# A convolutional row LSTM on one core: the work between the statistics and the first whole row is dealt out anew

## The chip, the core and the metric

The kernel runs on one core of a Trainium2 chip. The core has five engines that each work through a queue of their own in order: TensorE (PE in the profile, its weight loads PEld), VectorE (DVE), ScalarE (ACT), GpSimd (POOL) and SyncE (SP), which issues the transfers. They wait for each other on semaphores. The metric is the device time of one launch in microseconds; lower is better.

## The reference

The input `x` has 8 images of 96 channels and 128 x 128 pixels. The output is `x` plus a convolutional LSTM that runs over the 128 rows of each image from top to bottom, on the group-normalised input (32 groups of 3 channels, statistics over a whole image):

```python
its = lax.conv_general_dilated(X, W_is * mask, window_strides=(1, 1), padding=((0, 0), (1, 1)),
                               dimension_numbers=('NCHW', 'OIHW', 'NCHW')) + b_is[None, :, None, None]
def step(carry, row_in):
    h, c = carry
    ss = lax.conv_general_dilated(h, W_ss, window_strides=(1,), padding=((1, 1),),
                                  dimension_numbers=('NCW', 'OIW', 'NCW')) + b_ss[None, :, None]
    gates = ss + row_in
    g5 = gates.reshape(B, 3, 4, Oc, Wd)
    f, i, o = (jax.nn.sigmoid(g5[:, :, n].reshape(B, O, Wd)) for n in range(3))
    g = jnp.tanh(g5[:, :, 3].reshape(B, O, Wd))
    c_new = f * c + i * g
    h_new = o * jnp.tanh(c_new)
    return ((h_new, c_new), h_new)
_, hs = lax.scan(step, (h0, c0), xs)
return x + jnp.moveaxis(hs, 0, 2)   # X above is _gn(x)
```

A row can't begin before the row above it is done, so the rows are a chain of 128 steps. Both convolutions are three pixels wide along the row.

## The kernel before

**Half-steps.** The 8 images are two halves of 4, whose chains don't depend on each other. One row of one half is a half-step: half-step `n` is row `n // 2` of half `n % 2`, and there are 256 of them. While one half's products run on TensorE, the other half's gates run on ScalarE and VectorE. Four rows are a block. In the tile names the first digit behind the name is the half: `xs10` is half 1, buffer 0.

**Operands.** A row's even and odd pixels stand apart, and both convolutions are computed on sums and differences of neighbouring pixels. For the recurrent part these are made from the last hidden row `h`, which lies in `hx` beside 32 normalised input channels: the sum `vs` (step `S`, line 617) and the difference `vf` (step `F`, line 621), both on VectorE, and the shifted differences `vd` (step `D`, line 625) on GpSimd. `S` and `F` read two tiles in SBUF, as do all sums and differences here; the gates' VectorE instructions read one of their inputs from PSUM, where the products lie. For the other 64 input channels the sums and differences are made ahead of time, for whole blocks: `widen` (line 308 on ScalarE, 310 on GpSimd) normalises an image's 4 rows from `xr` into `xw`, `add_pixels` (line 327) writes the sums and `subtract_pixels` (line 331) the differences into `xs`. These three instructions on GpSimd are called an image below. The 32 channels in `hx` are normalised by `normalise_shared` (the same lines 308 and 310, written to `hx`).

**Products of a half-step.** The output channels come in three groups A, B and C of 128, one PSUM bank each. Group by group, `P` and `Q` are products with `xs`' sums and its first differences, `E` with its last ones; `1` and `2` take `vs` and `vf`, `0` and `3` take `vd`. Between them ScalarE copies the sum out (`cp`), and VectorE adds and subtracts the bank's halves (`lo`, `hi`). `E` of a group comes after its `lo`; `0` and `3` come after its `hi`. Then follow tanh (`ta`, line 555) and sigmoid (`si`), the products of the gates (`fg` for forget, line 572; `gt`, line 581), `ce`, `th`, the output `ou` that writes `h`, and the residual `re`, which adds `h` to `x`. A mark `+` or `*` behind a name means one or two half-steps ahead.

**Where the change acts.** The first 116 us read all of `x` for the statistics. Half-steps 0 and (in part) 2 already run beside that; the second half's last image comes last, and its scale is known at 135.3 us. From there to the regular rhythm the order is written out by hand: ScalarE widens rows 1 to 3 of block 0 of half 1 into `rows` (the buffer `piece0`), GpSimd normalises the shared channels of these rows and makes their sums and differences row by row (`own_row`), and `do(1, ...)` issues half-step 1 with the first products of half-steps 2 and 3. The residual of half-steps 0 and 1 runs on GpSimd. From half-step 2 on the string `PERIOD` sets the order, and GpSimd's share of each half-step comes from `work(n)`: normalised channels, one image for the next block, and a load. For the first 8 half-steps the table `FIRST` stands in for its rule; there the first image of half 1's block 1 is spread over three half-steps, in a second buffer `xw1`, and `LATER` spreads one image of block 2 over half-steps 9, 11 and 13.

**What a queue holds.** A wait on TensorE holds everything behind it in its queue. With 64 operand rows a product uses half of the array, and two such products run side by side in the two row groups; one with 128 rows needs both.

Of the kernel before, what the change touches and what calls it, by code (L numbers as in the profile page):

```python
# [21 lines left out]
def kernel(  # L22
# [29 lines left out]
    nc = tc.nc  # L52
    B, C, H, W = x.shape
    P = 128
    NH = 2
    BH = B // NH
    R = 4
    NB = H // R
    J = W // 2
# [80 lines left out]
    xw = [const.tile([P, R, W + 1], F32, tag=f"xw{i}", name=f"xw{i}") for i in range(2)]  # L140
# [11 lines left out]
    def rows_of(s, k, c0, c1, lo=0, hi=R):  # L152
        return x[s * BH : (s + 1) * BH, c0:c1, k * R + lo : k * R + hi, :].rearrange(
            "b c r w -> c b (r w)"
        )

    def load_rows(s, k, lo=0, hi=R):
        src = rows_of(s, k, 0, C2, lo, hi)
        for p in range(2):
            nc.sync.dma_start(xr[s][p * C2 : (p + 1) * C2, :, lo * W : hi * W], src)  # L160
# [10 lines left out]
    E = mybir.EngineType  # L171
# [140 lines left out]
    def widen(engine, xw, i, n, s, k, j, lo, step=1):  # L312


        return norm(
            engine,
            strided(xw[:, i, :], 0, [(step * (W + 1), n), (J + 1, 2), (1, J)]),
            xr[s][:, j, lo * W : (lo + n) * W]
            .rearrange("p (r j t) -> p r t j", r=n, t=2),
            0,  # L320
            1,
            s * BH + j,
        )

    def add_pixels(xw, n, total):

        nc.gpsimd.tensor_add(total, xw[:, 0:n, 0:J], xw[:, 0:n, J + 1 :])  # L327

    def subtract_pixels(xw, n, differences):

        nc.gpsimd.tensor_sub(  # L331
            differences,
            strided(xw[:, 0, :], 0, [(W + 1, n), (J, 2), (1, J)]),
            strided(xw[:, 0, :], J + 1, [(W + 1, n), (0, 2), (1, J)]),
        )

    def combine(xw, n, total, differences):

        add_pixels(xw, n, total)
        subtract_pixels(xw, n, differences)  # L340

    def own_image(s, k, j):

# [1 line left out]
        widen(nc.gpsimd, xw[0], 0, R, s, k, j, 0)  # L345
        combine(xw[0], R, to[:, :, 0, j, :], to[:, :, 1:3, j, :])

    def own_row(xw, s, r, lo=0, hi=BH):

        to = xs[s][0]  # L350
        combine(
            xw[:, lo:hi],
            hi - lo,
            to[:, r, 0, lo:hi],
            to[:, r, 1:3, lo:hi].rearrange("p t b j -> p b t j"),
        )

    def normalise_shared(engine, s, k, j, lo, hi):
# [17 lines left out]
    last = NT * NH - 1  # L376
# [63 lines left out]
    class HalfStep:  # L440
# [44 lines left out]
        def own(self, a, i):  # L485

            low = a == order["A"] or (a == order["C"] and (self.s == 0 or (self.n, i) == (1, 2)))
            rhs = self.xs[:, i].rearrange("p b j -> p (b j)")
            self.mm(a, i % 2, wo[i], rhs, slice(0, C2) if low else slice(C2, P))
# [94 lines left out]
        def part(self, ap, lo, hi, t=None):  # L584
            ap = ap.rearrange("p (t b j) -> p t b j", t=2, b=BH)
            return ap[:, :, lo:hi] if t is None else ap[:, t, lo:hi]
# [45 lines left out]
        def residual(self):  # L632
            s, row = self.s, self.row
            xo = xt[s, row // R][0:C, :, row % R, :].rearrange("p b (j t) -> p t b j", t=2)
            if self.n < NH or self.n == last - 1:
                nc.gpsimd.tensor_add(xo, xo, self.h)
            else:
                residuals.append(nc.vector.tensor_add(xo, xo, self.h))  # L638
# [21 lines left out]
    def shared(s, k, *images, engine=nc.gpsimd):  # L660
        parts = [j if isinstance(j, tuple) else (j, 0, R) for j in images]
        return [
            (normalise_shared, nc.scalar if hi == 1 else engine, s, k, j, lo, hi)
            for j, lo, hi in parts
        ]

    def beside(s, k, *images):
        return shared(s, k, *images, engine=nc.scalar)

    spread = own(1, 1, 0, 1)  # L670
    FIRST = [
        ([], own(0, 1, 0), []),
        (shared(0, 1, 0), own(0, 1, 1), []),
        (beside(0, 1, 1) + shared(0, 1, 2), own(0, 1, 2), []),
        (beside(0, 1, 3) + shared(1, 1, 0), own(0, 1, 3), [spread[0], (load_rows, 0, 2)]),
        (beside(1, 1, 1) + shared(1, 1, 2), own(1, 1, 1), [spread[1]]),
        (shared(1, 1, 3), own(1, 1, 2), [spread[2]]),
        ([], own(1, 1, 3), [(load_rows, 1, 2)]),
        ([], own(0, 2, 0), []),
    ]  # L680
    LATER = dict(zip((9, 11, 13), own(1, 2, 0, 1)))

    def work(n):
        if n < len(FIRST):
            return FIRST[n]
        row, s = divmod(n, NH)
        k, r = divmod(row, R)
        ahead, image = (k + 2, 0) if r == R - 1 else (k + 1, r + 1)
        return (
            shared(s, k + 1, *SHARED[r]) if k + 1 < NB else [],  # L690
            own(s, ahead, image) if ahead < NB else (),
            ([(load_rows, s, k + 2)] if r == R - 2 and k + 2 < NB else [])
            + ([LATER[n]] if n in LATER else []),
        )

    worked = {}
# [24 lines left out]
    def finish(n):  # L721
        prepare(n)
        row, s = divmod(n, NH)
        k, r = divmod(row, R)
        if r == R - 1:
            store(s, k, R - 1 if k + 1 == NB else 0, R)
            if k + 2 < NB:
                load(s, k + 2)
        elif r == R - 2 and k + 1 == NB:
            store(s, k, 0, R - 1)  # L730
# [26 lines left out]
    def half_step(n):  # L757
        if n not in steps:
            steps[n] = HalfStep(n)
        return steps[n]  # L760

    def do(n, names, by_lanes=False):

        for name in names.split():
            if name in "UX":
                if n >= NH:
                    prepare(n - NH, name)
                continue
            if name[0] == "W":
                prepare(n - 1 + name.count("+") - name.count("'"), name.strip("W+'"))  # L770
                continue
            at = n
            for mark, offset in (("'", -1), ("+", 1), ("*", 2)):
                at += offset * name.count(mark)
                name = name.replace(mark, "")
            images = None
            lane = "<>".find(name[-1]) if name[-1] in "<>" else None
            name = name.rstrip("<>")
            if name[0] in OWN and name[-1] in IMAGES:
                images, full = IMAGES[name[-1]], name[:-1]  # L780
# [39 lines left out]
    def shared_rows(engine, s, lo, hi, images=range(BH)):  # L820
        for j in images:
            normalise_shared(engine, s, 0, j, lo, hi)
# [97 lines left out]
    n = m = 0  # L920
# [38 lines left out]
    rows = ring[2][:, 0 : (R - 1) * BH * (W + 1)].rearrange("p (r q) -> p r q", q=W + 1)  # L959
# [28 lines left out]

    for j in range(BH):
        widen(nc.scalar, rows, j, R - 1, 1, 0, j, 1, step=BH)  # L990
    shared_rows(nc.gpsimd, 1, 1, R, range(0, 2))
    own_row(rows[:, 0:BH], 1, 1)
    shared_rows(nc.gpsimd, 1, 1, R, range(2, BH))
    for r in range(2, R):
        own_row(rows[:, (r - 1) * BH : r * BH], 1, r)
    load_rows(0, 1)
    for s in range(NH):
        load(s, 1)
    load_rows(1, 1)
# [2 lines left out]

    do(1, "1A 2A 1B 2B 1C 2C PA PB QA QB")
    half_step(1).images.clear()
    do(1, "E+A PC E+C QC P*A E+B cpA cpB cpC loA loB loC")
    do(1, "EA P*B Q*A EB EC Q*B hiB hiA hiC 0B 3B 0A 3A 0C 3C taB siB taA taC siC")
    finish(0)
    do(1, "gt th 0+A 3+A 0+B 3+B 0+C 3+C ou F S D re")
    finish(1)
# [65 lines left out]
```

## Time and profile before

| | us |
|---|---|
| median of 3 runs | 1966.7 |
| lowest, highest | 1965.13, 1968.21 |
| the profiled execution | 1967.33 |
| its span in the trace | 1965.5 |
| TensorE busy in the span | 1901.2 (97%) |
| VectorE, ScalarE, GpSimd busy | 1794.7, 1567.1, 1359.4 |

In the rows of the profile, "us from the span's start" comes first, then the duration, engine, line, operation and `out<-in` with partitions x elements; what ended the engine's idle time before the instruction stands in brackets at the end. One product shows up as two matmul records and two weight loads. An instruction's start can lie some tenths of a microsecond before it gets at its data, and consecutive ones of an engine can overlap by 0.1 us.

### The profile page before, as it was taken

To read this page: it belongs to the slowest core of one execution; us is meant where nothing else is said; L and a number is where in the kernel's file an instruction comes from. 1 tells how busy PE (TensorE), PEld (TensorE's weight loads), DVE (VectorE), ACT (ScalarE), POOL (GpSimd) and SP (SyncE) were. 2 spreads that over 40 slices of the span, in tenths; PEclk is the share of its full clock that TensorE was granted. 3 is DMA by queue.
4 is the path that set the end of the run, shared out by engine and by line. 5 is a ranking of instruction groups with operands and counts; after the bars stand their busy time and mean duration, and the time that the engine had idled before them with its cause. 6 is when DMAs were issued, how large, how long until landed. Compare 5 with 4: busy or idle time off the path is not lost.

```text
span 1965.5 us, 46244 instructions
## 1 busy us (share of the span) xinstructions
PE 1901.2 (97%) x17492; PEld 1819.2 (93%) x17492; DVE 1794.7 (91%) x4002; ACT 1567.1 (80%) x3494; POOL 1359.4 (69%) x1645
## 2 busy tenths in 40 slices
PE   3699999999999999999999999999999999999998
PEld 0279999999999999999999999999999999999997
DVE  5778999999999999999999999999999999999998
ACT  6777888887888888888888877888887888888777
POOL 3348777777777777777777777777777777777752
PEclk9999999999999999999999999999999999999999
DMA  9993343444334334433433443343344433434411
GB/s 402 421 308 75 88 116 94 105 119 117 82 87 115 97 98 119 119 90 85 107 98 98 119 119 98 82 103 100 95 119 119 101 86 95 109 94 112 119 34 33
DMA packets 101277, 234.64 MB, mean 119 GB/s; under 512 B 5824, under 2 KB 7360, under 8 KB 95040
## 3 DMA queue, kind: packets, MB, share of 16 engines
q1 hardware_dynamic: 101056, 231.70, 43.6%
q8 instruction: 138, 2.26, 0.5%
q14 instruction: 83, 0.68, 0.1%
HBM read 181.34 MB, written 50.33 MB: 118 GB/s over the span
## 4 chain that ended last, share of the span: by engine, by line
PE 93%; DMA 4%; DVE 2%; ACT 1%; issue 0%; SPq 0%; POOL 0%; DVEq 0%; POOLq 0%; ACTq 0%
PE ps L475 92%; DMA xs<-in_x_dram 4%; DVE bst L950 1%; PE ps L183 0%; PE dm L183 0%; ACT g L555 0%; ACT piece L308 0%; DVE ps L551 0%; DVE hx L604 0%; DVE ps L547 0%; SPq L938 0%; DVE vf L621 0%; PE rows L198 0%; ACT th L596 0%; ACT ps L567 0%
## 5 line engine op out<-in xcount | busy, mean ns | idle before, releaser
L475 PE MATMUL ps<-vd,wl 64*128 64x256 f32 (+1 forms) x6092 | 1191.6, 376 | 0.1
L475 PEld LDWEIGHTS ps<-vd,wl 64*128 64x128 f32 (+1 forms) x6092 | 871.9, 186 | 16.7 <-issue 1.3
L475 PE MATMUL ps<-vs,wm 64*128 64x256 f32 (+1 forms) x3054 | 821.3, 376 | 2.4 <-POOL vs L617 2.3
L475 PE MATMUL ps<-vf,wm 64*128 64x256 f32 (+1 forms) x3056 | 766.8, 377 | 1.1 <-DVE vf L621 1.1
L475 PE MATMUL ps<-xs,wx 64*128 64x256 f32 (+1 forms) x3586 | 747.1, 347 | 0.4 <-POOL xs L327 0.4
L475 PEld LDWEIGHTS ps<-xs,wx 64*128 64x128 f32 x3586 | 606.5, 187 | 4.3 <-POOL xs L327 2.3
L567 ACT ACTIVATE ps<-ps 96x256 f32<-96x256 f32 (+1 forms) x767 | 387.8, 506 | 231.5 <-PE ps L475 223.0
L475 PEld LDWEIGHTS ps<-vs,wm 64*128 64x128 f32 (+1 forms) x3054 | 528.8, 186 | 12.9 <-POOL vs L617 2.7
L555 ACT ACTIVATE g<-ps 32x256 f32<-32x256 f32 (+1 forms) x1021 | 468.6, 482 | 25.0 <-PE ps L475 6.0
L475 PEld LDWEIGHTS ps<-vf,wm 64*128 64x128 f32 (+1 forms) x3056 | 459.4, 186 | 20.9 <-DVE vf L621 1.9
L475 PE MATMUL ps<-xs,wt 64*128 64x256 f32 x1528 | 452.8, 377 | 0.4 <-DVE ps L551 0.4
L543 ACT ACTIVATE m<-ps,wl 128x256 f32<-128x256 f32 x766 | 363.0, 474 | 95.0 <-PE ps L475 70.1
L625 POOL TENSOR_TENSOR vd<-hx 128x512 f32<-128x512 f32 x257 | 287.9, 1120 | 180.0 <-DVE vs L617 170.3
L547 DVE TENSOR_TENSOR ps<-m,ps 128x256 f32<-128x256 f32 x768 | 324.3, 423 | 78.8 <-ACT m L543 78.6
L551 DVE TENSOR_TENSOR ps<-m,ps 128x256 f32<-128x256 f32 x768 | 326.9, 426 | 18.7 <-PE ps L475 1.2
L638 DVE TENSOR_TENSOR x<-x,hx 96x512 f32<-96x512 f32 x253 | 341.0, 1348 | 0.0
L310 POOL TENSOR_SCALAR xw<-xr,rstd,nmr 128x512 f32<-128x512 f32 (+1 forms) x255 | 205.6, 806 | 115.0 <-DVE x L638 114.5
L310 POOL TENSOR_SCALAR hx<-x,rstd,nmr 32x512 f32<-32x512 f32 (+1 forms) x249 | 222.4, 893 | 72.9 <-POOL xs L331 52.7
L331 POOL TENSOR_TENSOR xs<-xw 128x512 f32<-128x512 f32 (+1 forms) x254 | 270.9, 1067 | 0.0
L475 PEld LDWEIGHTS ps<-xs,wt 64*128 64x128 f32 x1528 | 266.5, 187 | 2.0 <-DVE ps L551 1.6
L579 POOL TENSOR_TENSOR g<-i,g 96x256 f32<-96x256 f32 x252 | 183.5, 728 | 118.0 <-ACT g L555 110.1
L604 DVE TENSOR_TENSOR hx<-ps,th 96x256 f32<-96x256 f32 (+1 forms) x510 | 190.5, 413 | 1.9 <-ACT th L596 1.8
(101 smaller groups left out, 1505.5 us busy)
## 6 DMA issues: line engine op xcount, KB each, us to landing
xr<-in_x_dram SPq DMA_DIRECT2D x124, 512.0 KB, 6.5
x<-in_x_dram SPq DMA_DIRECT2D x62, 768.0 KB, 5.9
out_dram<-x SPq DMA_DIRECT2D x62, 768.0 KB, 5.2
xs<-in_x_dram SPq DMA_DIRECT2D x31, 1024.0 KB, 12.4
piece<-in_x_dram SPq DMA_DIRECT2D x16, 1024.0 KB, 10.8
x<-in_x_dram SPq DMA_DIRECT2D x62, 256.0 KB, 3.2
out_dram<-x SPq DMA_DIRECT2D x2, 576.0 KB, 3.7
xs<-in_x_dram SPq DMA_DIRECT2D x2, 512.0 KB, 13.3
```

What stands on the lines that cost most here:

```text
L310: return engine.tensor_scalar(dst, src, scale, shift, ALU.mult, ALU.add)
L331: nc.gpsimd.tensor_sub(differences, strided(xw[:, 0, :], 0, [(W + 1, n), (J, 2), (1, J)]), strided(xw[:, 0, :], J + 1, [(W + 1, n), (0, 2) ...
L475: made = nc.tensor.matmul(self.ps[a][:, bass.ts(half, HB)][:, cols], weights[rows, bass.ts(a, P)], rhs[rows, cols], start=new, stop=False, ...
L543: nc.scalar.activation(self.m1[a], m1, AF.Identity, bias=column)
L547: nc.vector.tensor_add(self.ps[a][:, 0:HB], self.m1[a], self.ps[a][:, HB:])
L551: nc.vector.tensor_sub(hi, self.m1[a], hi)
L555: nc.scalar.activation(self.part(g, lo, hi, t), self.part(ps, lo, hi, t), AF.Tanh)
L567: nc.scalar.activation(to, gate, AF.Sigmoid)
L579: nc.gpsimd.tensor_mul(to, i, g)
L604: nc.vector.tensor_mul(h, o, th)
L625: diff = nc.gpsimd.tensor_sub(self.operand("vd", 2)[:, :, lo:hi], strided(h, 1, [(BH * JP - 1, 2), (JP, hi - lo), (1, J)]), strided(h, 0, ...
L638: residuals.append(nc.vector.tensor_add(xo, xo, self.h))
```

## The change

- Behind the statistics GpSimd no longer normalises the shared channels of rows 1 to 3 (four instructions on `hx`); ScalarE does, after the copies of half-step 1.
- GpSimd still makes row 1's sums and differences, but behind the first image of block 1 of half 0. Rows 2 and 3 are made by VectorE, ahead of half-step 1's gates.
- In half-step 1's products `EA EB EC` and the three `hi` come ahead of the four products of half-step 3 (`P*A P*B Q*A Q*B`), which read row 1.
- The residual of half-step 1 goes from GpSimd to VectorE.
- `FIRST` has six entries instead of eight. Three images of half 0's block 1 are made before half-step 2's work, the later ones come sooner, and none is spread; `LATER` and `spread` are gone. Half-steps 6 and 7 now follow the general rule, which makes the first images of block 2 there and normalises one image's shared channels that have been normalised before.

```diff
-            if self.n < NH or self.n == last - 1:
+            if self.n < 1 or self.n == last - 1:
                 nc.gpsimd.tensor_add(xo, xo, self.h)
             else:
                 residuals.append(nc.vector.tensor_add(xo, xo, self.h))
...
-    spread = own(1, 1, 0, 1)
     FIRST = [
-        ([], own(0, 1, 0), []),
-        (shared(0, 1, 0), own(0, 1, 1), []),
-        (beside(0, 1, 1) + shared(0, 1, 2), own(0, 1, 2), []),
-        (beside(0, 1, 3) + shared(1, 1, 0), own(0, 1, 3), [spread[0], (load_rows, 0, 2)]),
-        (beside(1, 1, 1) + shared(1, 1, 2), own(1, 1, 1), [spread[1]]),
-        (shared(1, 1, 3), own(1, 1, 2), [spread[2]]),
-        ([], own(1, 1, 3), [(load_rows, 1, 2)]),
-        ([], own(0, 2, 0), []),
+        ([], own(0, 1, 1), own(0, 1, 2)),
+        (shared(0, 1, 0), own(0, 1, 3), [(load_rows, 0, 2)]),
+        (beside(0, 1, 1) + shared(0, 1, 2), own(1, 1, 0), []),
+        (beside(0, 1, 3) + shared(1, 1, 0), own(1, 1, 1), []),
+        (beside(1, 1, 1) + shared(1, 1, 2), own(1, 1, 2), []),
+        (shared(1, 1, 3), own(1, 1, 3), [(load_rows, 1, 2)]),
     ]
-    LATER = dict(zip((9, 11, 13), own(1, 2, 0, 1)))
...
     for j in range(BH):
         widen(nc.scalar, rows, j, R - 1, 1, 0, j, 1, step=BH)
-    shared_rows(nc.gpsimd, 1, 1, R, range(0, 2))
+    load_rows(0, 1)
+    for part, *args in own(0, 1, 0):
+        part(*args)
     own_row(rows[:, 0:BH], 1, 1)
-    shared_rows(nc.gpsimd, 1, 1, R, range(2, BH))
-    for r in range(2, R):
-        own_row(rows[:, (r - 1) * BH : r * BH], 1, r)
-    load_rows(0, 1)
...
-    do(1, "E+A PC E+C QC P*A E+B cpA cpB cpC loA loB loC")
-    do(1, "EA P*B Q*A EB EC Q*B hiB hiA hiC 0B 3B 0A 3A 0C 3C taB siB taA taC siC")
+    do(1, "E+A PC E+C QC E+B cpA cpB cpC loA loB loC")
+    shared_rows(nc.scalar, 1, 1, R)
+    do(1, "EA EB EC hiA hiB hiC P*A P*B Q*A Q*B")
+    for r in range(2, R):
+        own_row(rows[:, (r - 1) * BH : r * BH], 1, r, engine=nc.vector)
+    do(1, "0B 3B 0A 3A 0C 3C taB siB taA taC siC")
```

`own_row`, `combine`, `add_pixels` and `subtract_pixels` get the engine as an argument, with GpSimd as its default.

The order on TensorE, from `QC` of half-step 1 to its first product with `vd`, before (`wx` are the weights of `P` and `Q`, `wt2` those of `E`; `ps0`, `ps1`, `ps2` are the banks of A, B, C, and `ps0_1_1` that of half 1, row 1, which is half-step 3):

```order
L475 MATMUL ps2_1_0_775<-xs10_76,wx_67 128x256
L475 MATMUL ps0_1_1_786<-xs10_76,wx_67 128x256
L475 MATMUL ps1_0_1_550<-xs00_74,wt2_65 128x256
L475 MATMUL ps0_1_0_546<-xs10_76,wt2_65 128x256
L475 MATMUL ps1_1_1_799<-xs10_76,wx_67 128x256
L475 MATMUL ps0_1_1_786<-xs10_76,wx_67 128x256
L475 MATMUL ps1_1_0_547<-xs10_76,wt2_65 128x256
L475 MATMUL ps2_1_0_775<-xs10_76,wt2_65 128x256
L475 MATMUL ps1_1_1_799<-xs10_76,wx_67 128x256
L475 MATMUL ps1_1_0_547<-vd_1_0_664,wl_64 128x256 x2
```

The same stretch of TensorE's queue after the change:

```order
L476 MATMUL ps2_1_0_770<-xs10_76,wx_67 128x256
L476 MATMUL ps1_0_1_550<-xs00_74,wt2_65 128x256
L476 MATMUL ps0_1_0_546<-xs10_76,wt2_65 128x256
L476 MATMUL ps1_1_0_547<-xs10_76,wt2_65 128x256
L476 MATMUL ps2_1_0_770<-xs10_76,wt2_65 128x256
L476 MATMUL ps0_1_1_801<-xs10_76,wx_67 128x256
L476 MATMUL ps1_1_1_803<-xs10_76,wx_67 128x256
L476 MATMUL ps0_1_1_801<-xs10_76,wx_67 128x256
L476 MATMUL ps1_1_1_803<-xs10_76,wx_67 128x256
L476 MATMUL ps1_1_0_547<-vd_1_0_664,wl_64 128x256 x2
```

The four products of half-step 3 stood among half-step 1's three `E`; now they stand in one piece behind them and right ahead of `vd`.

GpSimd's queue from the end of half-step 1's `vd` to the first image of the next block, before (`hx10` shared channels, `piece0` the widened rows 1 to 3, `xs10` and `xs01` the sums and differences of half 1's block 0 and half 0's block 1):

```order
L625 TENSOR_TENSOR vd_1_0_664<-hx10_72 128x2x64
L310 TENSOR_SCALAR hx10_72<-x1_0_153,rstd1_104,nmr1_106 32x3x2x64 x2
L327 TENSOR_TENSOR xs10_76<-piece0_113 128x256
L331 TENSOR_TENSOR xs10_76<-piece0_113 128x4x2x64
L310 TENSOR_SCALAR hx10_72<-x1_0_153,rstd1_104,nmr1_106 32x3x2x64 x2
L327 TENSOR_TENSOR xs10_76<-piece0_113 128x256
L331 TENSOR_TENSOR xs10_76<-piece0_113 128x4x2x64
L327 TENSOR_TENSOR xs10_76<-piece0_113 128x256
L331 TENSOR_TENSOR xs10_76<-piece0_113 128x4x2x64
L310 TENSOR_SCALAR xw0_80<-xr0_78,rstd0_103,nmr0_105 128x4x2x64
```

The same stretch of GpSimd's queue after the change:

```order
L626 TENSOR_TENSOR vd_1_0_664<-hx10_72 128x2x64
L310 TENSOR_SCALAR xw0_80<-xr0_78,rstd0_103,nmr0_105 128x4x2x64
L327 TENSOR_TENSOR xs01_75<-xw0_80 128x4x64
L331 TENSOR_TENSOR xs01_75<-xw0_80 128x4x2x64
L327 TENSOR_TENSOR xs10_76<-piece0_113 128x256
L331 TENSOR_TENSOR xs10_76<-piece0_113 128x4x2x64
L310 TENSOR_SCALAR xw0_80<-xr0_78,rstd0_103,nmr0_105 128x4x2x64
```

An image takes the place of the first two `hx` instructions; rows 2 and 3 are gone, and two more images follow row 1 (the last row is the first of them) before `vd` of half-step 3.

VectorE's queue from `hiC` of half-step 1 to the forget product of half-step 2, before:

```order
L551 TENSOR_TENSOR ps2_1_0_775<-m2_1_0_793,ps2_1_0_775 128x256
L581 TENSOR_TENSOR c1_83<-ps1_1_0_547,g_1_0_814 96x512
L604 TENSOR_TENSOR hx10_72<-ps2_1_0_775,th_1_0_824 96x2x4x64
L621 TENSOR_TENSOR vf_1_1_833<-hx10_72 128x256
L617 TENSOR_TENSOR vs_1_1_835<-hx10_72 128x256
L572 TENSOR_TENSOR ps0_0_1_548<-ps0_0_1_548,c0_82 96x512
```

The same stretch of VectorE's queue after the change:

```order
L552 TENSOR_TENSOR ps2_1_0_770<-m2_1_0_786,ps2_1_0_770 128x256
L327 TENSOR_TENSOR xs10_76<-piece0_113 128x256
L331 TENSOR_TENSOR xs10_76<-piece0_113 128x4x2x64
L327 TENSOR_TENSOR xs10_76<-piece0_113 128x256
L331 TENSOR_TENSOR xs10_76<-piece0_113 128x4x2x64
L582 TENSOR_TENSOR c1_83<-ps1_1_0_547,g_1_0_817 96x512
L605 TENSOR_TENSOR hx10_72<-ps2_1_0_770,th_1_0_830 96x2x4x64
L622 TENSOR_TENSOR vf_1_1_839<-hx10_72 128x256
L618 TENSOR_TENSOR vs_1_1_841<-hx10_72 128x256
L639 TENSOR_TENSOR x1_0_153<-x1_0_153,hx10_72 96x2x4x64
L573 TENSOR_TENSOR ps0_0_1_548<-ps0_0_1_548,c0_82 96x512
```

Rows 2 and 3 of `xs10` came in ahead of `gt` (line 581 before, 582 after), and the residual behind `S`.

More of the change, by code (lines that the diff above doesn't have):

```diff
@@ L323, in widen, with add_pixels, subtract_pixels @@
         )
[L325 to L331, printed above, removed]
+    def add_pixels(xw, n, total, engine=nc.gpsimd):
+        engine.tensor_add(total, xw[:, 0:n, 0:J], xw[:, 0:n, J + 1 :])
+    def subtract_pixels(xw, n, differences, engine=nc.gpsimd):
+        engine.tensor_sub(
             differences,
@@ L335, in subtract_pixels, with combine @@
         )
-    def combine(xw, n, total, differences):
-        add_pixels(xw, n, total)
-        subtract_pixels(xw, n, differences)
+    def combine(xw, n, total, differences, engine=nc.gpsimd):
+        add_pixels(xw, n, total, engine)
+        subtract_pixels(xw, n, differences, engine)
     def own_image(s, k, j):
@@ L346, in own_image, with own_row @@
         combine(xw[0], R, to[:, :, 0, j, :], to[:, :, 1:3, j, :])
-    def own_row(xw, s, r, lo=0, hi=BH):
+    def own_row(xw, s, r, lo=0, hi=BH, engine=nc.gpsimd):
         to = xs[s][0]
@@ L355, in own_row @@
             to[:, r, 1:3, lo:hi].rearrange("p t b j -> p b t j"),
+            engine,
         )
@@ L691, in work @@
             own(s, ahead, image) if ahead < NB else (),
-            ([(load_rows, s, k + 2)] if r == R - 2 and k + 2 < NB else [])
-            + ([LATER[n]] if n in LATER else []),
+            [(load_rows, s, k + 2)] if r == R - 2 and k + 2 < NB else [],
         )
```

## The prediction

> **What bounds the kernel now.** I read the stretches of the span first, then the chain of work that ended last, then each engine's instructions in order of time around the change. The table by stretch (busy time of each engine, then the granted clock):
>
> ```profile
> core 0: us, PE busy (x) PEld busy (x) DVE busy (x) ACT busy (x) POOL busy (x), PEclk, DMA share, GB/s
> 128.00:142.00 14.00, 13.63 (x96) 10.89 (x94) 8.06 (x26) 5.27 (x10) 5.28 (x12) 1.00 1.00 205
> 142.00:157.00 15.00, 13.90 (x90) 11.56 (x88) 9.07 (x21) 10.13 (x22) 13.70 (x17) 1.00 0.26 54
> 157.00:172.00 15.00, 14.89 (x140) 14.27 (x140) 13.32 (x32) 12.57 (x28) 13.54 (x15) 1.00 0.34 72
> 172.00:400.00 228.00, 227.96 (x2168) 222.29 (x2168) 213.01 (x479) 184.91 (x424) 170.20 (x194) 1.00 0.40 100
> 400.00:1900.00 1500.00, 1500.00 (x14303) 1468.33 (x14302) 1404.97 (x3155) 1212.06 (x2785) 1094.88 (x1259) 1.00 0.41 101
> ```
>
> From 157 us on TensorE has no gap (1500.00 of 1500) at full clock; there the change leaves its matmuls as they are. So the change can act in two ways only: it can let the seamless stretch begin earlier or later than 157.11, or open gaps in the half-steps after it. TensorE's idle time that could be won between 128 and 157 is 0.37 + 1.10 us. These rows hold nearly all of it (the third is of the weight loads), and the work beside it:
>
> ```profile
> 139.99 0.48 PE L475 MATMUL ps<-xs,wx 64*128 64x256 f32 x1 [0.37 <-POOL xs L327]
> 148.82 0.70 PE L475 MATMUL ps<-vf,wm 64*128 64x256 f32 x4 [0.25 <-DVE vf L621]
> 141.02 0.18 PEld L475 LDWEIGHTS ps<-xs,wx 64*128 64x128 f32 x1 [0.29 <-POOL xs L331]
> 142.28 5.45 PE L475 MATMUL ps<-vd,wl 128*128 128x256 f32 x24
> 147.66 0.92 PE L475 MATMUL ps<-xs,wx 64*128 64x256 f32 x6
> 153.16 1.17 PE L475 MATMUL ps<-vd,wl 64*128 64x256 f32 x7
> 155.90 0.38 PE L475 MATMUL ps<-xs,wx 64*128 64x256 f32 x1
> 157.11 0.70 PE L475 MATMUL ps<-vf,wm 64*128 64x256 f32 x4 [0.83 <-DVE vf L621]
> ```
>
> TensorE waits once for GpSimd's row 1 and twice for VectorE's difference `F` (L621), each the first operand of a new half-step. GpSimd and VectorE over the same time:
>
> ```profile
> 137.40 1.50 POOL L310 TENSOR_SCALAR hx<-x,rstd,nmr 32x384 f32<-32x384 f32 x2
> 139.30 0.64 POOL L327 TENSOR_TENSOR xs<-piece 128x256 f32<-128x256 f32 x1 [0.40 <-ACT piece L308]
> 139.90 1.07 POOL L331 TENSOR_TENSOR xs<-piece 128x512 f32<-128x512 f32 x1
> 147.42 1.07 POOL L331 TENSOR_TENSOR xs<-xw 128x512 f32<-128x512 f32 x1
> 149.25 1.04 POOL L625 TENSOR_TENSOR vd<-hx 128x512 f32<-128x512 f32 x1 [0.76 <-DVE vs L617]
> 150.24 1.30 POOL L636 TENSOR_TENSOR x<-x,hx 96x512 f32<-96x512 f32 x1
> 151.53 0.80 POOL L310 TENSOR_SCALAR xw<-xr,rstd,nmr 128x512 f32<-128x512 f32 x1
> 152.41 0.64 POOL L327 TENSOR_TENSOR xs<-xw 128x256 f32<-128x256 f32 x1
> 154.18 0.85 POOL L310 TENSOR_SCALAR xw<-xr,rstd,nmr 128x512 f32<-128x512 f32 x1
> 155.71 1.06 POOL L331 TENSOR_TENSOR xs<-xw 128x512 f32<-128x512 f32 x1
> 158.08 1.35 POOL L625 TENSOR_TENSOR vd<-hx 128x512 f32<-128x512 f32 x1
> ```
>
> ```profile
> 140.18 0.43 DVE L547 TENSOR_TENSOR ps<-m,ps 128x256 f32<-128x256 f32 x1 [0.16 <-ACT m L543]
> 141.79 1.09 DVE L551 TENSOR_TENSOR ps<-m,ps 128x256 f32<-128x256 f32 x3 [1.19 <-PE ps L475]
> 145.91 0.69 DVE L581 TENSOR_TENSOR c<-ps,g 96x512 f32<-96x512 f32 x1 [3.02 <-ACT g L555]
> 148.08 0.69 DVE L621 TENSOR_TENSOR vf<-hx 128x256 f32<-128x256 f32 x1
> 148.69 0.41 DVE L617 TENSOR_TENSOR vs<-hx 128x256 f32<-128x256 f32 x1
> 151.68 0.43 DVE L547 TENSOR_TENSOR ps<-m,ps 128x256 f32<-128x256 f32 x1 [1.97 <-ACT m L543]
> 155.83 1.22 DVE L621 TENSOR_TENSOR vf<-hx 128x256 f32<-128x256 f32 x1
> 157.64 0.90 DVE L638 TENSOR_TENSOR x<-x,hx 96x512 f32<-96x512 f32 x1
> ```
>
> Here is the point on which the sum turns. `F` and `S` are alike, 256 elements from two SBUF inputs, and `S` took 0.41. But `F` took 0.69 beside a GpSimd subtraction that ended at 148.49, and 1.22 beside one that ended at 156.77: both end 0.28 later. So such a VectorE instruction waits until GpSimd's running instruction is over. It holds the other way too: `vd` took 1.35 instead of 1.04 behind the residual of 157.64. The gap of 0.83 at 157.11 is this wait: `F` would have ended at 156.26, and TensorE's earlier work ended at 156.28 (155.90 + 0.38).
>
> **The change, part by part.** The profiled execution took 1967.33 us, 1.8 more than its span; the median of the runs is 0.6 below it.
>
> *Row 1 behind an image, and TensorE's new order.* On GpSimd two `hx` instructions (1.50) leave and one image comes ahead of row 1; an image is 2.65 from start to start (151.53 to 154.18). From 137.40 the image ends near 139.96, and row 1's two instructions near 140.6 and 141.6, 0.66 later than now (140.97). Now `Q*A` waits for that subtraction (the row of 141.02), `EB` stands behind it, `hiB` waits for `EB` (1.19), and `0B` for `hiB`: 142.28. After the change `EA EB EC` wait only for `loA loB loC`, the last over at 140.61, and `hiC` is done near 141.8. `P*` and `Q*` now stand ahead of `0B`: `Q*` starts near 141.7 and clears both row groups near 142.15. That is 0.13 earlier. Bounds: 0.66 later (the lateness in full) to 0.4 earlier (`0B` right behind `hiB`); I take the worked value, since every duration in it has a row.
>
> *Four `hx` on ScalarE.* The nearest rows are its four widenings of the same 384 elements, and the idle time that has to cover them:
>
> ```profile
> 136.10 3.05 ACT L308 ACTIVATE piece<-xr,nmr,rstd 128x384 f32<-128x384 f32 x4
> 143.44 0.59 ACT L555 ACTIVATE g<-ps 32x512 f32<-32x512 f32 x1 [3.30 <-PE ps L475]
> ```
>
> From 140.14, when `cpC` is over (the VectorE row of 140.18 waits for it), 3.05 reach 143.19; the tanh they stand before can start at 143.31. Hidden, with 0.12 to spare; bounds 0 to 0.2 late.
>
> *Rows 2 and 3 on VectorE.* Two instructions of 256 and two of 512 elements, behind `hiC` (141.8) and ahead of `gt` (145.91 now, 145.80 then). Alone they are 2 x 0.41 + 2 x 0.68 = 2.2, the 0.68 from this row (its shortest, where GpSimd was idle):
>
> ```profile
> L638 DVE TENSOR_TENSOR x<-x,hx x253: 683/1512/1517, 157.6 to 1961.4; 96x512 f32<-96x512 f32 x127
> ```
>
> But beside them GpSimd works through two images without a gap, and all four read two SBUF tiles. Taking turns, each holds the other up: 0.28 or 0.56 for VectorE's (what `F` needed once free, and twice that), 0.7 to 0.8, 0.64 and 1.07 for GpSimd's three. If VectorE's first addition starts first, the end is 141.8 + 0.28 + 0.75 + 0.56 + 0.64 + 0.28 + 1.07 + 0.56 = 145.9, which is on time within 0.1. If GpSimd's widening goes first, 0.8 more: 146.7, and `gt` is 0.9 late. The two starts lie within 0.1 of each other (141.73 and 141.78), and I take VectorE first: the widening of 151.53 took 0.80, yet the next instruction began 0.88 after it, so a widening seems to reach its data late.
>
> The Trainium skill, page "SBUF — State Buffer", section "Who interferes with whom", speaks against this part of the change: a VectorE instruction with two SBUF inputs and a GpSimd instruction that reads SBUF exclude each other for a whole instruction, and whichever starts first decides who waits. The trace agrees with the 0.69, 1.22 and 1.35 above. Without the rule the four would be over at 144.0 and this part could cost nothing in any order.
>
> *`F` of the next half-step.* With `gt` 0.11 earlier `F` is ready at 147.97. GpSimd's second image ends near 148.15 (145.9 + 0.7 + 0.64 + 1.07, less overlaps of some 0.1), so `F` waits a little and ends near 148.43. TensorE's earlier work ends at 148.58 - 0.13 = 148.45. The start of `vf` moves from 148.82 to 148.45: 0.37 won.
>
> *The residual on VectorE.* 0.68 between `S` and the forget product, in 1.97 of idle time: nothing. Behind it GpSimd's `vd` takes 1.35 and ends near 150.25, as now (150.29); TensorE wants it at 153.16. Queued behind are the images, which no longer wait for 1.30 of residual: two of them end near 155.45 instead of 156.77. `F` of half-step 4 comes 7.01 after the start of `vf` (148.82 to 155.83), at 155.46, so it finds GpSimd just free and ends at 155.9. TensorE's work before it ends at 156.28 - 0.37 = 155.91. The seamless stretch starts at 155.93 instead of 157.11: **1.2 us earlier**, the 0.37 included.
>
> *The later half-steps.* Images come a half-step or two sooner; the spread ones go; two needless `hx` of 384 elements (0.75 each) are added at half-steps 8 and 9, as the shortened list hands these over to the general rule. GpSimd is idle for 58 of the 228 us after 172: nothing. The rows that the image at 137.40 widens are loaded in time: this transfer was issued behind the one of 114.62 and took at most 18.2, so it was over by 134.2:
>
> ```profile
> 114.62 1.36 SPq L160 DMA_DIRECT2D xr<-in_x_dram  x2
> DMA to landing us min/median/max: 5.1/7.0/18.2
> ```
>
> Sum: 1967.33 - 1.2 = 1966.1 for this execution, 1965.5 for a median like the one shown. That is 0.06%, and a measurement of this kernel can tell about 0.2% (3.9 us) from no change.
>
> **Rivals.** *GpSimd takes the first turn at 141.73.* `gt` is 0.9 late, `F` ends at 149.33, `vf` starts 0.55 later than now. `F` of half-step 4 then finds GpSimd free, because the images, held up too, end near 156.4, where it starts, and the stretch begins near 156.85: 0.3 won, 1966.4. The two starts are so close that the trace hardly speaks against it.
>
> *`F` of half-step 4 still meets a subtraction.* GpSimd's second image after `vd` need only be 0.1 later than worked out. Up to 0.8 of the gain is lost: 1966.3. With the rival before, 0.5 us more than now: 1967.2.
>
> *Slower: `F` meets GpSimd in half-step after half-step.* Room is small, as half-step 5 shows: `F` ends at 164.19, and TensorE starts on it at 164.34.
>
> ```profile
> 163.76 0.43 DVE L621 TENSOR_TENSOR vf<-hx 128x256 f32<-128x256 f32 x1
> 164.34 0.69 PE L475 MATMUL ps<-vf,wm 64*128 64x256 f32 x4
> ```
>
> Half-steps 5 to 13 get other GpSimd lists. Were each `F` there caught behind a subtraction, from a wait of 0.15 on, each costs up to the 0.83 of 157.11: 9 x 0.83 = 7.5, less 1.2, makes 1973.0 on the median. Against it: from half-step 16 on GpSimd's list per half-step is the one that now comes at 4 already (`vd`, an image, `gt`, one `hx`), and with it TensorE has no gap in 1500 us.
>
> *More is won than 0.2%.* All of TensorE's idle time from 128 to 157 is 1.47 us; more than that would need less matmul work. Almost excluded.
>
> **How the numbers follow.** Likeliest, 0.50: 1965.5. GpSimd first, 0.20: 1966.4. A subtraction met at half-step 4, with or without the former, 0.17: 1966.3 to 1967.2. Repeated stalls, 0.08: 1968 to 1973. A gain past 0.2%, 0.05, for what I may have overlooked. The first three lie within 0.2%: 0.87. The range takes in the three runs' own spread of 3 us, 1.8 below the likeliest and 0.8 above the worst of the second and third case: 1963.7 to 1968.0.
>
> **What would show it.** In the profile after: four `hx` on ScalarE ending before 143.3; VectorE's rows 2 and 3 stretched to near 1 us each, with `gt` starting by 145.9; `0B` near 142.15; `F` near 148 of at most 0.5; `F` of half-step 4 near 155.5 of about 0.43, and TensorE without a gap from 155.9. I am wrong if `gt` starts after 146.5, if `F` is again over 1 us there, or if TensorE waits for `F`, `vd` or `xs` anywhere past 160.

## The result and the profile after

The changed kernel takes 1963.43 us (median of 22 runs, 1962.66 to 1966.30), the kernel before 1966.53 (22 runs, 1964.95 to 1968.31). The ratio is 0.9987, with a 95% interval of 0.9982 to 0.9993: 0.13% faster, too little for the 0.2% that was set as what a measurement can tell, but outside its own interval. The median of 1963.43 lies 0.3 us below the predicted range and 2.1 below the predicted 1965.5.

The profiled execution after took 1964.65 us, its span 1962.8. Of the same stretches as before, these are the ones that carry the change (busy time of each engine, then the clock):

```profile
core 0: us, PE busy (x) PEld busy (x) DVE busy (x) ACT busy (x) POOL busy (x), PEclk, DMA share, GB/s
128.00:142.00 14.00, 14.00 (x95) 11.65 (x95) 8.91 (x29) 7.03 (x14) 5.99 (x12) 1.00 0.96 200
142.00:157.00 15.00, 14.96 (x102) 12.48 (x101) 12.37 (x26) 11.74 (x24) 13.22 (x14) 1.00 0.57 121
172.00:400.00 228.00, 228.00 (x2177) 223.41 (x2176) 213.21 (x481) 185.02 (x426) 166.95 (x192) 1.00 0.41 102
```

TensorE's idle time between 128 and 157, 1.47 us before, is down to 0.04. Two executions can't be compared by times from the span's start alone, because the statistics end at another time in each. The instruction that ends them is `nmr` on GpSimd, in the trace of before, in order of time:

```profile
135.46 0.20 POOL L971 TENSOR_TENSOR nmr<-minus,rstd 128x2 f32<-128x2 f32 x1 [7.29 <-DVE rstd L299]
```

The same instruction after, with TensorE's first `vd` product and its first `vf` products of half-steps 3 and 4:

```profile
135.68 0.20 POOL L967 TENSOR_TENSOR nmr<-minus,rstd 128x2 f32<-128x2 f32 x1 [7.31 <-DVE rstd L299]
...
142.36 5.45 PE L476 MATMUL ps<-vd,wl 128*128 128x256 f32 x24
...
148.58 0.70 PE L476 MATMUL ps<-vf,wm 64*128 64x256 f32 x4
...
156.07 0.70 PE L476 MATMUL ps<-vf,wm 64*128 64x256 f32 x4
```

From here on times of the start are counted from the end of `nmr` (135.66 before, 135.87 after, from unrounded times). On that count `vd` moved from 6.62 to 6.49, `vf` of half-step 3 from 13.16 to 12.71 and `vf` of half-step 4 from 21.45 to 20.20: 0.13, 0.45 and 1.25 us won, where 0.13, 0.37 and 1.18 had been forecast.

GpSimd and VectorE side by side in the profile after, in order of time; the last three rows are the two `F` and the subtraction that ends ahead of the second:

```profile
140.61 1.07 POOL L331 TENSOR_TENSOR xs<-piece 128x512 f32<-128x512 f32 x1
141.67 0.80 POOL L310 TENSOR_SCALAR xw<-xr,rstd,nmr 128x512 f32<-128x512 f32 x1
141.95 0.80 DVE L327 TENSOR_TENSOR xs<-piece 128x256 f32<-128x256 f32 x1
142.55 0.69 POOL L327 TENSOR_TENSOR xs<-xw 128x256 f32<-128x256 f32 x1
142.67 1.13 DVE L331 TENSOR_TENSOR xs<-piece 128x512 f32<-128x512 f32 x1
143.21 1.51 POOL L331 TENSOR_TENSOR xs<-xw 128x512 f32<-128x512 f32 x1
143.72 1.28 DVE L327 TENSOR_TENSOR xs<-piece 128x256 f32<-128x256 f32 x1
144.82 1.38 POOL L310 TENSOR_SCALAR xw<-xr,rstd,nmr 128x512 f32<-128x512 f32 x1
144.92 0.68 DVE L331 TENSOR_TENSOR xs<-piece 128x512 f32<-128x512 f32 x1
145.99 0.69 DVE L582 TENSOR_TENSOR c<-ps,g 96x512 f32<-96x512 f32 x1 [0.39 <-ACT g L556]
148.10 0.43 DVE L622 TENSOR_TENSOR vf<-hx 128x256 f32<-128x256 f32 x1
154.48 1.07 POOL L331 TENSOR_TENSOR xs<-xw 128x512 f32<-128x512 f32 x1
155.59 0.43 DVE L622 TENSOR_TENSOR vf<-hx 128x256 f32<-128x256 f32 x1
```

Both `F` now take 0.43 instead of 0.69 and 1.22; the second starts 0.04 behind the end of GpSimd's subtraction. The four stretched VectorE rows (0.80, 1.13, 1.28, 0.68 for work that takes 0.41 and 0.68 alone) are over at 145.60, and `gt` behind them waits for the tanh, not for them.

That is 1.25 us. Compared group by group (the groups of runs are in the last section), the runs show about 2.2, and the rest lies later. TensorE's first `vf` product of half-steps 6, 7, 8, 13, 14, 15 and 16, before:

```profile
171.48 0.69 PE L475 MATMUL ps<-vf,wm 64*128 64x256 f32 x4
...
178.99 0.70 PE L475 MATMUL ps<-vf,wm 64*128 64x256 f32 x4
...
186.22 0.69 PE L475 MATMUL ps<-vf,wm 64*128 64x256 f32 x4
...
221.88 0.69 PE L475 MATMUL ps<-vf,wm 64*128 64x256 f32 x4
...
229.40 0.69 PE L475 MATMUL ps<-vf,wm 64*128 64x256 f32 x4
...
236.53 0.69 PE L475 MATMUL ps<-vf,wm 64*128 64x256 f32 x4
...
243.75 0.69 PE L475 MATMUL ps<-vf,wm 64*128 64x256 f32 x4
```

Half-steps 6, 7 and 8 after the change:

```profile
170.43 0.69 PE L476 MATMUL ps<-vf,wm 64*128 64x256 f32 x4
...
177.56 0.69 PE L476 MATMUL ps<-vf,wm 64*128 64x256 f32 x4
...
184.69 0.69 PE L476 MATMUL ps<-vf,wm 64*128 64x256 f32 x4
```

From one such start to the next it is 7.13 after, in every half-step from 6 to 16. Before, half-steps 7, 8, 14 and 16 took 7.51, 7.23, 7.52 and 7.22: together 0.96 us of stall in a stretch in which the profile of before had TensorE busy for 227.96 of 228 us. How it hides there, and what makes it, is seen at 170 to 172 (before; GpSimd, VectorE, then TensorE's first product with `vs`, which follows the `vf` row of 171.48):

```profile
170.06 0.65 POOL L327 TENSOR_TENSOR xs<-xw 128x256 f32<-128x256 f32 x1
170.81 1.05 POOL L310 TENSOR_SCALAR hx<-x,rstd,nmr 32x512 f32<-32x512 f32 x1
...
170.90 0.45 DVE L621 TENSOR_TENSOR vf<-hx 128x256 f32<-128x256 f32 x1
171.27 0.87 DVE L617 TENSOR_TENSOR vs<-hx 128x256 f32<-128x256 f32 x1
...
172.19 0.48 PE L475 MATMUL ps<-vs,wm 64*128 64x256 f32 x1
```

The same place after, with the `vf` row at 170.43:

```profile
169.16 0.80 POOL L310 TENSOR_SCALAR hx<-x,rstd,nmr 32x512 f32<-32x512 f32 x1
...
170.18 0.42 DVE L618 TENSOR_TENSOR vs<-hx 128x256 f32<-128x256 f32 x1
...
170.86 0.38 PE L476 MATMUL ps<-vs,wm 64*128 64x256 f32 x1
```

Before, the addition of the spread image (170.06) stands ahead of GpSimd's `hx`. It pushes `hx` next to `F` and `S`; `F` goes first, then `hx`, and `S` ends 0.28 behind the end of `hx` (171.86), in 0.87 instead of 0.42. TensorE's first product with `vs` starts 0.71 behind that with `vf` instead of 0.43. In the busy time nothing of this is seen, because the four matmul records of 171.48 are drawn to end at 172.17, 0.02 ahead of the late one. The Trainium skill, page "Perfetto Trace Analysis", opens by calling matmul busy time a bad metric for how close a kernel is to its limit, because matmuls are pipelined. This trace bears that out, with 0.38 us lost in a half-step that reads as fully busy.

### The profile page after: what moved, and what is told of

Its sections match the earlier page's. It is cut to its first block, busy times and chain, and to the rows that moved or that the text cites. A ratio compares the mean times of both kernels' runs of the same rounds, so it can differ in the third digit from the quotient of the medians.

```text
span 1962.8 us, 46242 instructions
## 1 busy us (share of the span) xinstructions
PE 1902.6 (97%) x17492; PEld 1823.2 (93%) x17492; DVE 1797.2 (92%) x4007; ACT 1567.9 (80%) x3498; POOL 1348.9 (69%) x1638
## 4 chain that ended last, share of the span: by engine, by line
PE 93%; DMA 4%; DVE 1%; ACT 0%; issue 0%; SPq 0%; DVEq 0%; ACTq 0%
PE ps L476 93%; DMA xs<-in_x_dram 4%; DVE bst L946 1%; PE ps L183 0%; PE dm L183 0%; SPq L934 0%; PE rows L198 0%; PE rows L183 0%; PE pv L264 0%; PE dm L264 0%; DVE ps L552 0%; ACT g L556 0%; ACT ps L568 0%; ACT th L597 0%; DVE ps L548 0%
## 5 line engine op out<-in xcount | busy, mean ns | idle before, releaser
L310 POOL TENSOR_SCALAR hx<-x,rstd,nmr 32x512 f32<-32x512 f32 x247 | 219.3, 888 | 75.9 <-POOL xs L331 51.8
```

The lines of the kernel that those rows point to most:

```text
L310: return engine.tensor_scalar(dst, src, scale, shift, ALU.mult, ALU.add)
```

## Experiments

Two theories were set against each other, for each part of the gain. **T**: 1.25 us come from the start, of which 0.8 from the residual's move (it frees `F` of half-step 4 from GpSimd's subtraction), and 0.96 from the spread images, whose addition makes `S` wait for `hx`. **Rivals**: the order of TensorE's products or the images made ahead carry the start, and the later gain has another cause than the spread. All times in the table are counted from the end of `nmr` of that execution, in us; the last columns are the profiled execution's whole time less the end of `nmr`, and the ratio of the runs to those of before, with its interval.

| | end of `nmr` | first `vd` | `vf` 3 | `vf` 4 | `vf` 16 | rest | ratio |
|---|---|---|---|---|---|---|---|
| before | 135.66 | 6.62 | 13.16 | 21.45 | 108.09 | 1831.67 | |
| after | 135.87 | 6.49 | 12.71 | 20.20 | 105.86 | 1828.78 | 0.9987 [0.9982, 0.9993] |
| after_one_spread | 134.03 | 6.49 | 12.71 | 20.20 | 106.34 | 1829.38 | 0.9989 [0.9980, 0.9998] |
| before_no_late_addition | 137.29 | 6.62 | 13.14 | 21.43 | 107.67 | 1830.69 | 0.9997 [0.9988, 1.0005] |
| spread_with_hx_on_scalare | 137.29 | 6.49 | 12.70 | 20.19 | 105.96 | 1828.77 | 0.9994 [0.9984, 1.0003] |
| after_residual_on_gpsimd | 134.32 | 6.49 | 12.71 | 21.02 | 106.69 | 1829.69 | 0.9988 [0.9979, 0.9996] |
| before_residual_on_vectore | 134.42 | 6.61 | 13.13 | 20.62 | 107.23 | 1830.19 | 0.9993 [0.9984, 1.0002] |
| after_rows_on_gpsimd | 133.98 | 6.50 | 12.85 | 21.54 | 107.23 | 1830.46 | 0.9998 [0.9989, 1.0007] |
| after_order_of_before | 135.66 | 7.11 | 13.33 | 20.82 | 106.50 | 1829.70 | 0.9995 [0.9985, 1.0004] |
| before_order_of_after | 135.78 | 6.49 | 13.11 | 21.40 | 108.01 | 1830.83 | 1.0000 [0.9990, 1.0009] |

The ratios can't tell these kernels apart; their intervals are some 3 us wide. The starts in the traces can: kernels that share a stage agree in it within 0.03 us (`vd` at 6.49 or 6.50 in six of them).

### One image spread again

```diff
+    LATER = dict(zip((9, 11, 13), own(1, 2, 0, 1)))
...
-            own(s, ahead, image) if ahead < NB else (),
-            [(load_rows, s, k + 2)] if r == R - 2 and k + 2 < NB else [],
+            own(s, ahead, image) if ahead < NB and n != 7 else (),
+            ([(load_rows, s, k + 2)] if r == R - 2 and k + 2 < NB else [])
+            + ([LATER[n]] if n in LATER else []),
```

> The changed kernel, but the first image of half 1's block 2 is not made whole at half-step 7: its three instructions are spread over half-steps 9, 11 and 13 as before the change. Times between the starts of TensorE's first vf product of two half-steps that follow each other. Theory T (the unforeseen gain of 0.96 us at half-steps 7, 8, 14 and 16 comes from the spread images, whose addition pushes GpSimd's hx so late that VectorE's S stands behind it): half-step 14 takes 7.51 again instead of 7.13 and half-step 16 takes 7.22, while 7 and 8 stay at 7.13; 0.48 us more than the changed kernel. Rival R (the gain there comes from the earlier images or the new order at the start, and the spread ones are as free as predicted): every half-step from 6 on stays at 7.13, and nothing is lost.

Half-steps 7 and 8 stayed at 7.13, 14 took 7.51 and 16 took 7.23; `vf` of half-step 16 came 0.48 later than after the change. `hx`, `S` and the `vf` products of half-steps 13 and 14, in this kernel's order of time:

```profile
217.84 1.04 POOL L310 TENSOR_SCALAR hx<-x,rstd,nmr 32x512 f32<-32x512 f32 x1
...
218.30 0.86 DVE L618 TENSOR_TENSOR vs<-hx 128x256 f32<-128x256 f32 x1
...
218.51 0.69 PE L476 MATMUL ps<-vf,wm 64*128 64x256 f32 x4
...
226.02 0.69 PE L476 MATMUL ps<-vf,wm 64*128 64x256 f32 x4
```

The stall of before is back in the place and the size that T gave, with the whole start of the change kept. The spread image is its cause at half-steps 14 and 16, and the rival falls.

### The addition of that image left out

```diff
     LATER = dict(zip((9, 11, 13), own(1, 2, 0, 1)))
+    del LATER[11]
```

> The kernel before, without the addition of the spread image of block 2 (one GpSimd instruction of 128x256 in half-step 11's list is left out, and the sums of that image with it); its widening and its subtraction stay. T (it is the addition's place right ahead of hx that costs): half-step 14 takes 7.13 instead of 7.52, its S at the half-step before 0.42 instead of 0.87; half-steps 7 (7.52), 8 (7.23) and 16 (7.22) stay as before; 0.39 us less than before. Rival (the widening, the subtraction or the second buffer costs, or something else at that time): half-step 14 keeps its 7.52.

Half-step 14 took 7.13, while 7, 8 and 16 kept 7.51, 7.23 and 7.23; `vf` of half-step 16 came 0.42 earlier than before. `S` and the `vf` products of half-steps 13 and 14:

```profile
223.23 0.42 DVE L617 TENSOR_TENSOR vs<-hx 128x256 f32<-128x256 f32 x1
...
223.48 0.69 PE L475 MATMUL ps<-vf,wm 64*128 64x256 f32 x4
...
230.61 0.69 PE L475 MATMUL ps<-vf,wm 64*128 64x256 f32 x4
```

One GpSimd instruction of 0.64 us, on an engine that is idle a quarter of the time there, cost TensorE 0.38. The widening and the buffer cost nothing at half-step 14.

### The addition kept, the `hx` behind it given to ScalarE

On top of `after_one_spread`:

```diff
-            shared(s, k + 1, *SHARED[r]) if k + 1 < NB else [],
+            shared(s, k + 1, *SHARED[r], engine=nc.scalar if n == 10 else nc.gpsimd)
+            if k + 1 < NB else [],
```

> The changed kernel with one image of block 2 spread over half-steps 9, 11 and 13 (as in after_one_spread), and the one hx instruction that stands behind the spread addition in GpSimd's queue is given to ScalarE. T (S waits for that hx, which the addition has pushed to the same time as F and S): S ahead of half-step 14 takes 0.42 instead of 0.86 and half-step 14 takes 7.13 instead of 7.51, with the addition still there; half-step 16 keeps 7.22. Rival 1 (the addition itself holds S or TensorE up): half-step 14 keeps 7.51. Rival 2 (ScalarE, idle for 1.03 there, becomes late by the hx): half-step 14 between 7.2 and 7.6 with S at 0.42.

The `hx` took 0.85 on ScalarE, and half-step 14 took 7.13:

```profile
220.62 0.85 ACT L308 ACTIVATE hx<-x,nmr,rstd 32x512 f32<-32x512 f32 x1
...
221.51 0.42 DVE L618 TENSOR_TENSOR vs<-hx 128x256 f32<-128x256 f32 x1
...
221.76 0.69 PE L476 MATMUL ps<-vf,wm 64*128 64x256 f32 x4
...
228.89 0.69 PE L476 MATMUL ps<-vf,wm 64*128 64x256 f32 x4
```

So it is not the addition that `S` waits for but the `hx` that it pushes: both rivals fall. Half-step 16 kept 7.23, and only 0.10 us separate this kernel from the changed one.

### The residual of half-step 1, each way

In the changed kernel, and the reverse edit in the kernel before:

```diff
-            if self.n < 1 or self.n == last - 1:
+            if self.n < NH or self.n == last - 1:
```

> The changed kernel with the residual of half-step 1 on GpSimd again. T (as predicted: the 1.30 of residual made GpSimd's second image end so late that F of half-step 4 waited for its subtraction): the images end near 156.85 instead of 155.55, F there takes some 1.2 to 1.5 instead of 0.43, and half-step 4 takes about 8.5 instead of 7.49, so about 1.0 us is lost. Rival (F is free there because three images are made ahead, wherever the residual runs): half-step 4 stays at 7.49.

> The kernel before with only the residual of half-step 1 moved to VectorE. T: the start of vf at half-step 3 stays where it was, GpSimd's second image behind vd ends near 155.5 instead of 156.77, F of half-step 4 takes 0.43 instead of 1.22, and half-step 4 takes 7.46 instead of 8.29: 0.8 us won; half-steps 7, 8, 14 and 16 stay at 7.52, 7.23, 7.52 and 7.22. Rival (the images made ahead are what frees F): half-step 4 stays near 8.29.

`F` of half-step 4 and the `vf` behind it, in the changed kernel with the residual on GpSimd:

```profile
154.04 1.24 DVE L622 TENSOR_TENSOR vf<-hx 128x256 f32<-128x256 f32 x1
...
155.34 0.70 PE L476 MATMUL ps<-vf,wm 64*128 64x256 f32 x4 [0.85 <-DVE vf L622]
```

The same in the kernel before with the residual on VectorE:

```profile
154.56 0.43 DVE L621 TENSOR_TENSOR vf<-hx 128x256 f32<-128x256 f32 x1
...
155.04 0.70 PE L475 MATMUL ps<-vf,wm 64*128 64x256 f32 x4
```

Half-step 4 took 8.31 instead of 7.49 in the first (0.2 less than expected, since GpSimd's images had ended a little earlier), and 7.49 instead of 8.29 in the second. The move alone is worth 0.8 us in either kernel, and the images made ahead don't free `F`. After the change `F` starts only 0.04 behind the end of the subtraction, but that thin margin repeats: half-step 4 took 7.49 or 7.50 in five kernels.

### Rows 2 and 3 back on GpSimd

```diff
-        own_row(rows[:, (r - 1) * BH : r * BH], 1, r, engine=nc.vector)
+        own_row(rows[:, (r - 1) * BH : r * BH], 1, r)
```

> The changed kernel with rows 2 and 3 of half 1's block 0 made by GpSimd (behind row 1) instead of VectorE. Times from the end of nmr, the last of the statistics: in the changed kernel the first vd product starts at 6.49, gt at 10.12, and vf of half-steps 3 and 4 at 12.71 and 20.20. Theory T (GpSimd's lateness reaches TensorE only through F): vd stays at 6.49 and gt at 10.12; GpSimd's next two images come 3.3 later, F of half-step 3 meets the third image's widening, vf of half-step 3 starts near 13.0; the two images behind vd end near 21.1, F of half-step 4 is caught and vf starts near 21.4: 1.2 us lost. Rival: GpSimd's idle time before vd (1.08) and behind the images takes most of it, and vf of half-step 4 starts before 20.5.

`vd` and `gt` stayed at 6.50 and 10.13. `vf` of half-step 3 lost 0.14 and that of half-step 4 lost 1.35. These are `S` behind the `F` of half-step 3, then `F` and `vf` of half-step 4:

```profile
146.69 0.86 DVE L618 TENSOR_TENSOR vs<-hx 128x256 f32<-128x256 f32 x1
...
154.18 1.28 DVE L622 TENSOR_TENSOR vf<-hx 128x256 f32<-128x256 f32 x1
...
155.52 0.70 PE L476 MATMUL ps<-vf,wm 64*128 64x256 f32 x4 [0.89 <-DVE vf L622]
```

The rival falls, and T's times came near, but not its "only through F". `S` took 0.86 beside GpSimd's addition instead of 0.42, and `F` of half-step 4 started 7.36 behind `vf` of half-step 3 (146.82) instead of 7.01. So 0.35 of the loss came ahead of that `F`, most likely through `S`, which was not tried by itself; the other 0.86 is `F`'s own wait for the subtraction. With the images made ahead and rows 2 and 3 still on GpSimd, the residual's move wins nothing at half-step 4 (8.70, against 8.29 before the change); in the kernel before, which makes fewer images ahead, it won 0.8 with these rows on GpSimd.

### TensorE's order, each way

In the changed kernel the order of before, and in the kernel before the order of after:

```diff
-    do(1, "E+A PC E+C QC E+B cpA cpB cpC loA loB loC")
+    do(1, "E+A PC E+C QC P*A E+B cpA cpB cpC loA loB loC")
...
-    do(1, "EA EB EC hiA hiB hiC P*A P*B Q*A Q*B")
+    do(1, "EA P*B Q*A EB EC Q*B hiB hiA hiC")
```

> The changed kernel with the order of TensorE's products of before: the four products of half-step 3 stand among half-step 1's three E again. T (Q*A waits for row 1's subtraction, which now ends at 5.81 behind nmr instead of 5.31, and EB, hiB and 0B wait behind it): the first vd product starts near 7.1 instead of 6.49, vf of half-step 3 near 13.3 instead of 12.71 and of half-step 4 near 20.8 instead of 20.20: 0.6 us lost. Rival (the order is free, since VectorE's other work or the tanh hides it): vd within 0.2 of 6.49.

> The kernel before with only TensorE's products of half-steps 1 and 3 in the new order. T: the first vd product starts at 6.49 behind nmr instead of 6.62, gt at 10.1, but F of half-step 3 still waits for GpSimd's subtraction, so vf stays near 13.1 and that of half-step 4 near 21.4: less than 0.1 us won by the order alone. Rival (the order carries the 0.45 won at half-step 3): vf of half-step 3 near 12.7.

The changed kernel with the order of before started `vd` at 7.11, and all that follows came 0.62 later. The kernel before with the new order started it at 6.49, yet `vf` of half-step 3 came only 0.04 earlier, because `F` was caught all the same:

```profile
148.06 0.77 DVE L621 TENSOR_TENSOR vf<-hx 128x256 f32<-128x256 f32 x1
...
148.88 0.70 PE L475 MATMUL ps<-vf,wm 64*128 64x256 f32 x4 [0.33 <-DVE vf L621]
```

The new order wins next to nothing alone. It is what lets row 1 come later without a price: `vd` starts at 6.49 whether row 1's subtraction ends 5.29 behind `nmr`, as here, or 5.81, as after the change. So no single part carries the 0.45 of half-step 3: it takes the new order and an `F` that GpSimd leaves free.

## Why the prediction was right in its steps and short in its sum

**Row 1 and TensorE's order**: right in the time, 0.13 of 0.13. The prediction derived it from the end of row 1's subtraction, which it expected 0.66 later. That end came 0.50 later (5.81 behind `nmr` instead of 5.31), and the kernel before with the new order starts `vd` at the same 6.49 without that lateness, so TensorE's own products set the start. The prediction's upper bound, the lateness in full, is what the old order shows: there `vd` comes 0.49 later than before the change (7.11 against 6.62).

**Four `hx` on ScalarE**: right. They ran from 140.38 to 143.4 and the tanh behind them started at 143.53, 7.66 us behind `nmr`; it was at 143.44 before (7.78).

**Rows 2 and 3 on VectorE**: the taking of turns was right, the order and one price weren't. GpSimd's widening had the first turn: it started at 141.67, VectorE's addition at 141.95. Less the 0.21 by which `nmr` was later, VectorE came at 141.74 as forecast (141.73), and GpSimd at 141.46 instead of 141.78. That is the condition of the first rival, which had the rows end at 146.7 and `gt` 0.9 late. In fact they ended at 145.60, which is 145.39 on the prediction's scale, even ahead of the 145.9 forecast for the other case. What failed is the price of 0.8 that the rival set for one more GpSimd turn: VectorE's last two instructions (143.72 and 144.92) ran one after the other, and the second image's widening, which would have had its turn between them, waited until both were over (144.82, in 1.38 instead of 0.80). `gt` waited 0.39 for the tanh, so up to that much lateness would have been free. That `gt` came on time was in part luck: the turn that the forecast chose did not come, and the rival's price for the other turn was too high.

**`F` of half-steps 3 and 4**: right. 0.45 against 0.37, then 0.80 against 0.81. The forecast had the first `F` wait a little; it did not wait, because GpSimd's image ended at 147.95, 0.15 ahead of it. The rival in which it still meets a subtraction missed by 0.04 us, from the end of the subtraction of 154.48 (155.55) to the start of `F` (155.59).

**The later half-steps**: this is the step that failed. "The spread ones go" was costed at nothing, because GpSimd is idle for 58 of 228 us there and TensorE has no gap. Their removal won 0.96 us: 0.38 each at half-steps 7 and 14, where the addition pushes `hx` in front of `S`, and 0.1 each at 8 and 16, where the kernel before had `F` in 0.52 instead of 0.43 (at 178.42 and 235.94; it comes and goes with the spread image, but that it is the spread subtraction that `F` meets was not tried by itself). The runs show this for block 2's image, at half-steps 14 and 16. No run takes away block 1's spread image by itself, so the 0.48 at 7 and 8 rests on the rows at 170 and on the same sizes. The same reading of busy time made the prediction say that more than TensorE's 1.47 us of idle time "would need less matmul work"; 2.2 us were won with the same matmuls (17492 records in either trace). The two needless `hx` did cost nothing: every half-step from 6 on takes 7.13.

**The sum**: 0.45 + 0.80 + 0.96 = 2.21 against a forecast of 1.18. At half-step 16 the two kernels lie 2.23 apart. Of the 2.1 by which the median fell below the forecast, 1.0 is this difference; the rest is mostly the mix of the groups of runs, which the last section shows. Counted from `nmr`, the two profiled executions differ by 2.9 in all. The other 0.67 can't be put down to the change: it grows evenly over the 239 half-steps behind, at 7.1337 us each before and 7.1309 after. The kernels made from before take 7.1305 to 7.1312 there, and those made from after 7.1305 to 7.1322. What makes one execution slower by 0.04% all along is open.

**The slower rival** (repeated stalls at half-steps 5 to 13) did not come: no `F` from half-step 4 to 16 takes over 0.43. Stalls of that family, VectorE behind GpSimd in later half-steps, were in the kernel before, and there it was mostly `S` behind `hx`, which the prediction had not looked at.

## What to carry to other kernels

A bound engine that reads as fully busy can still lose tenths of a microsecond per step: compare the starts of the same instruction from step to step, and treat every period that differs from the rest as a stall to be explained. When work is taken off an engine with idle time, ask what that work pushes, not how busy the engine is; here a 0.64 us instruction cost 0.38 because of the instruction queued behind it. To measure such a change, count from an event behind the noisy stage, not from the launch.

## What was not expected of the hardware

**The runs come in three groups, 1.6 us apart.** Of the changed kernel 12 runs lie at 1962.7 to 1963.4, 6 at 1964.5 to 1964.7 and 4 at 1966.0 to 1966.3; of the kernel before 9 at 1965.0 to 1965.6, 9 at 1966.4 to 1966.8 and 4 at 1968.2 to 1968.3. Group by group the medians differ by 2.23, 1.96 and 2.17 us, which is the sum above; the medians of all runs differ by 3.1 because the lowest group is larger after. In the ten traces the end of `nmr` falls in three groups as well (134.0 to 134.4, 135.7 to 135.9, 137.3), and the rest of the time doesn't follow them. So the spread arises in the first 137 us. Why the statistics end at three different times wasn't tried.

**A tenth of a microsecond decides who waits.** GpSimd's `hx` that started 0.09 ahead of `F` (170.81 and 170.90) let `F` pass, then ran ahead of `S`, which took 0.87. One that starts 0.06 behind `F`, at 155.65 in the profile after, took 1.30 and let both pass: `S` there took 0.42. An instruction of GpSimd with one SBUF input besides its scales is enough to hold up a VectorE instruction with two. The Trainium skill, page "SBUF — State Buffer", section "Who interferes with whom", has such a pair contend, and these rows agree. The same section lets the order of issue decide who waits; the starts in the profile don't show that order within 0.1 us (the `hx` of 170.81 has the earlier start, yet `F` passed), and no run here settles why `S` passed as well in the second case.
